# Two attention blocks with pooled keys on one core: parameter vectors loaded as rows, the bias of g carried through W, small PSUM banks for some visits, and the order of the last copies

## The chip, the cores and the metric

One core of one Trainium2 chip runs the whole program. The metric is the device time of one execution in microseconds (us), the median of several runs. The engines named below are PE (TensorE, matrix products; PEld is its weight load), DVE (VectorE), ACT (ScalarE), POOL (GpSimd) and SP (SyncE, which here only issues transfers). PSUM is the memory that PE writes to; the kernel divides its eight banks among three pools.

## The reference

`x` has the shape 4 x 128 x 96 x 96 (batch, channels, height, width), all in fp32. Two layers of the same form follow one another; for each image b with N = 9216 pixels, and with CI = 64:

- g = maxpool2(g_w x + g_b), phi = maxpool2(phi_w x + phi_b), each 64 x 2304 (the pool takes 2 x 2 pixels); theta = theta_w x + theta_b, 64 x 9216
- f = theta^T phi, a 9216 x 2304 matrix of scores; attn = softmax of f over the 2304 keys
- y = attn g^T, back to 64 x 9216
- the output is (W_w y + W_b) * inv + (bn_beta - bn_mean * inv) + x, with inv = bn_gamma / sqrt(bn_var + 1e-5)

The output of layer 0 is the input of layer 1. The parameters of each layer are three matrices 64 x 128 (g_w, phi_w, theta_w), one 128 x 64 (W_w), and vectors: three of 64 elements (g_b, theta_b, phi_b) and five of 128 (W_b, bn_gamma, bn_beta, bn_mean, bn_var). phi_b adds the same to all scores of a pixel and drops out of the softmax. A constant added to g passes the weighted mean of the softmax unchanged.

## The kernel before

`nonlocal_blocks` runs `shifted_blocks`, which takes a fixed shift of 35 from the scores in place of each row's maximum, and then, only if a flag says that the sums of exponentials left the safe range, `general_blocks`. With these inputs the second function isn't run.

**Blocks and pairs.** A block is one image in one layer; `ORDER` (line 41) sets the order of the eight blocks. Each block has nine pairs; a pair is two query tiles of 512 pixels, one on the upper and one on the lower half of the partitions, so there are 72 pairs, numbered through. The 2304 keys make 18 key tiles, two of which are one step; a pair has nine steps. The order of instructions on PE, DVE, ACT and SP is the order of the program (line 77).

**The main loop** (lines 476 to 511). At step t, `scores` (line 276) of the two key tiles of this step: eight products (sixteen instructions, since each fp32 product is two passes) into a large PSUM tile of two banks (pool `ps_sc`, two such tiles), and on ACT the exponential, whose sums DVE adds up (line 292). Then `values` (line 294) of the step before. After the first values of a pair comes the "window": first up to two of the `others`, steps that prepare the next block; then the **visit** (line 429); then the rest of the others; then `normalise`. The visit takes one large tile for two things: the denominators of the pair before (line 313) in its first bank and the theta of the next pair (line 267) in its second; ACT then empties both, the denominators with a running sum (line 323), theta with its bias (line 274). At the fifth step `project` (line 343) multiplies the normalised pair before by W in the two small tiles of one bank each (pool `ps_misc`, used in rotation), and DVE adds the shift and x (line 356).

**The others.** `pooled` (line 200) computes g and phi of 384 pixels, one chunk, in a small tile, and DVE takes their maximum. `spread` (line 242) turns six or three key tiles: on ACT the centred phi, and on PE the transposes of g into a small tile, which DVE adds g's bias to on the way to `gT` (line 235). `key_steps` (line 246) gives the windows of a block their others: with three chunks a window, eight windows have three chunks (two of them a `spread` as well) and the ninth has one `spread` alone. For the second block there are four chunks a window from the third window on, none in the first two, and a `spread` alone in the ninth. In the last block no window has others. The first block's own keys are prepared before the loop and between its first steps.

**The start** (lines 397 to 460). ACT's queue issues g_w, theta_w, theta_b twice as a column, both variances as columns, g_b spread to all partitions, W_w and four rows of vectors. SP's queue issues phi_w and the twelve pieces of the first image, then the parameters of layer 1. PE multiplies the identity eight times as a warm-up (line 445), transposes the weights, and takes chunks 0 to 3, theta of pair 0 (`visit(-1)`), and chunks 4 to 7. ACT takes the square roots of both variances and then loads the table of the exponential. `make_shift` and `make_W` (lines 155 to 169) of layer 0 come at steps 6 and 7, those of layer 1 at steps 18 and 19.

**The end** (`finish`, line 363, for pair 71). `take_denominators` lets DVE take the reciprocals straight out of PSUM and ACT sum the denominators; ACT then copies half of the values (line 368), DVE adds the halves and multiplies, PE projects, and DVE and SP write four pieces. `check` and `result` set the flag in between.

Of the kernel before, what the change touches and what calls it, by code (L numbers as in the profile page):

```python
# [16 lines left out]
P = 128  # L17
# [19 lines left out]
J_WINDOW, J_PROJECT = 0, 4  # L37
CHUNKS = 3
FIRST_CHUNKS, FIRST_GT = 4, 3
WARM = 8  # L40
ORDER = ((0, 0), (1, 0), (0, 1), (2, 0), (1, 1), (3, 0), (2, 1), (3, 1))
SHIFT = 35.0
SUM_MIN, SUM_MAX = 1e-20, 1e30
# [3 lines left out]
def shifted_blocks(ctx: ExitStack, tc: tile.TileContext, x: bass.AP, layers, out: bass.AP, flag):  # L47
# [46 lines left out]
            nc.sync.dma_start(out=xt[:, ts(i, HW // n)], in_=src[:, ts(i, HW // n)])  # L94
        return xt

    def as_column(src):
        return src.rearrange("(c o) -> c o", o=1)

    def as_row(src):  # L100
        return src.rearrange("(o c) -> o c", o=1)

# [9 lines left out]
    class Layer:  # L112


        def __init__(self, l, p):
            self.l, self.p = l, p

        def load_gphi(self, engines):
            self.gphi_nat = prep.tile([2 * CI, C], F32, name=f"gphi_nat_{self.l}")
# [3 lines left out]
        def load_theta(self, engine):  # L123
            self.theta_nat = prep.tile([CI, C], F32, name=f"theta_nat_{self.l}")
            engine.dma_start(out=self.theta_nat, in_=self.p["theta_w"])
            self.theta_b = const.tile([2 * CI, 1], F32, name=f"theta_b_{self.l}")
            for i in range(2):
                engine.dma_start(out=self.theta_b[ts(i, CI), :], in_=as_column(self.p["theta_b"]))

        def load_var(self, engine):  # L130
            self.var = prep.tile([C, 1], F32, name=f"var_{self.l}")
            engine.dma_start(out=self.var, in_=as_column(self.p["bn_var"]))

        def load_g_b(self, engine):
            self.g_b = const.tile([P, CI], F32, name=f"g_b_{self.l}")
            engine.dma_start(out=self.g_b, in_=as_row(self.p["g_b"]).to_broadcast((P, CI)))

        def load_W(self, engine):
            self.W_nat = prep.tile([C, CI], F32, name=f"W_nat_{self.l}")
            engine.dma_start(out=self.W_nat, in_=self.p["W_w"])  # L140
            self.rows = prep.tile([4, C], F32, name=f"rows_{self.l}")
            for i, key in enumerate(("W_b", "bn_gamma", "bn_beta", "bn_mean")):
                engine.dma_start(out=self.rows[i : i + 1, :], in_=as_row(self.p[key]))

        def make_std(self):
            self.std = prep.tile([C, 1], F32, name=f"std_{self.l}")
            nc.scalar.activation(self.std, self.var, AF.Sqrt, bias=eps)

        def make_gphi(self):
            self.gphi = transposed(self.gphi_nat, 2 * CI, C, f"gphiT_{self.l}")  # L150
# [1 line left out]
        def make_theta(self):  # L152
            self.theta = transposed(self.theta_nat, CI, C, f"thetaT_{self.l}")

        def make_shift(self):
            cols = transposed(self.rows, 4, C, f"cols_{self.l}")
            W_b, gamma, beta, mean = (cols[:, i : i + 1] for i in range(4))
            inv = prep.tile([C, 1], F32, name=f"inv_{self.l}")
            nc.vector.reciprocal(inv, self.std)
            nc.vector.tensor_mul(inv, inv, gamma)  # L160
            shift = const.tile([C, 1], F32, name=f"shift_{self.l}")
            nc.vector.tensor_sub(shift, W_b, mean)
            nc.vector.scalar_tensor_tensor(shift, shift, inv, beta, op0=ALU.mult, op1=ALU.add)
            self.shift = shift
            self.W_bn = prep.tile([C, CI], F32, name=f"W_bn_{self.l}")
            nc.vector.tensor_scalar(self.W_bn, self.W_nat, inv, None, ALU.mult)

        def make_W(self):
            self.W = transposed(self.W_bn, C, CI, f"WT_{self.l}", twice=True)

    class Block:

# [54 lines left out]
        def spread_g(self, i):  # L227

            gt = self.gt
            ps = ps_misc.tile([P, QT], F32, tag="misc", name=f"gT_ps_{self.name}_{i}")  # L230
            for j in range(gt):
                nc.tensor.transpose(
                    ps[:, ts(j, CI)], self.gphi[:CI, ts(i * gt + j, KT)], ident[:CI, :CI]
                )
            nc.vector.tensor_tensor(
                self.gT[:, ts(i, gt), :],
                ps[:, : gt * CI].rearrange("p (t c) -> p t c", c=CI),
                self.w.g_b.rearrange("p (o c) -> p o c", o=1).to_broadcast((P, gt, CI)),
                ALU.add,
            )  # L240

        def spread(self, i):
# [13 lines left out]
    class Pair:  # L256
# [14 lines left out]

        def take_theta(self, ps):
            self.th = work.tile([P, QT], F32, tag="theta", name=f"theta_{self.name}")
            nc.scalar.activation(self.th, ps, AF.Identity, bias=self.blk.w.theta_b)  # L274

        def scores(self, k):
            ps = ps_sc.tile([P, PT], F32, tag="sc", name=f"sc_{self.name}_{k}")
# [38 lines left out]
                    )  # L316

        def take_denominators(self, ps):
            self.rc = work.tile([P, QT], F32, tag="rc", name=f"rc_{self.name}", bufs=1)
            if self.last:  # L320
                self.inverses(ps)
            n = self.number
            nc.scalar.activation(  # L323
                self.th if self.last else self.rc, ps, AF.Identity,
                accum_out=dens[:, n : n + 1],
            )

        def inverses(self, src):
            for i in range(QT // P):
# [33 lines left out]
        def finish(self, check, result):  # L363

            n = QT // 2
            halves = work.tile([P, PT], F32, tag="halves", name=f"halves_{self.name}", bufs=1)
            y, half = halves[:, :QT], halves[:, QT:]
            nc.scalar.copy(half, self.av[:, QT:])
            nc.vector.tensor_add(y, self.av[:, :QT], half)
            for i in range(2):  # L370
                nc.vector.tensor_mul(y[:, ts(i, n)], y[:, ts(i, n)], self.rc[:, ts(i, n)])
            self.note()
            pss = [
                ps_sc.tile([P, PT], F32, tag="sc", name=f"W_ps_{self.name}_{i}") for i in range(2)
            ]
            for i in range(2):
                for c in range(2):
                    for h in range(2):
                        nc.tensor.matmul(
                            pss[i][ts(c, CI), h * QT : h * QT + n],  # L380
                            lhsT=self.blk.w.W[ts(h, CI), ts(c, CI)],
                            rhs=y[ts(h, CI), ts(i, n)], start=True, stop=True,
                        )
            check()
            for i in range(2):
                for h in range(2):
                    first = (2 * self.p + h) * QT + i * n
                    dst = self.blk.xt[:, first : first + n]
                    nc.vector.scalar_tensor_tensor(
                        dst, pss[i][:, h * QT : h * QT + n], self.blk.w.shift, dst,  # L390
                        op0=ALU.add, op1=ALU.add,
                    )
                    nc.sync.dma_start(out=self.blk.store[:, first : first + n], in_=dst)
                if i == 0:
                    result()
# [2 lines left out]
    ws[0].load_gphi((nc.scalar, nc.sync))  # L398
    xs = {0: load_x(0, 12)}
    ws[0].load_theta(nc.scalar)  # L400
    for w in ws:
        w.load_var(nc.scalar)
    ws[0].load_g_b(nc.scalar)
    ws[0].load_W(nc.scalar)
    for w in ws:
        w.make_std()
    nc.scalar.preload_act_table(AF.Exp)
    ws[1].load_gphi((nc.sync, nc.sync))
    ws[1].load_theta(nc.sync)
    ws[1].load_g_b(nc.sync)  # L410
    ws[1].load_W(nc.sync)

    blocks = []
# [12 lines left out]
    pairs = [Pair(blk, p, n * NP + p) for n, blk in enumerate(blocks) for p in range(NP)]  # L426
    total = len(pairs) * NB

    def visit(n):

        ps = ps_sc.tile([P, PT], F32, tag="sc", name=f"den_theta_ps_{n}")
        den, th = ps[:, :QT], ps[:, QT:]
        if n > 0:
            pairs[n - 1].denominators(den)
        if n + 1 < len(pairs):
            pairs[n + 1].theta(th)
        if n > 0:
            pairs[n - 1].take_denominators(den)
        if n + 1 < len(pairs):
            pairs[n + 1].take_theta(th)  # L440
# [3 lines left out]
    for i in range(WARM):  # L444
# [7 lines left out]
    b0.pooled(0)  # L452
    b0.pooled(1)
    b0.pooled_2(2)
    b0.spread_phi(0)
    visit(-1)
    b0.pooled(4)
# [8 lines left out]
        2: [lambda: b0.spread_phi(3), lambda: b0.spread_g(3)],  # L466
        4: [lambda: b0.spread_phi(4), lambda: b0.spread_g(4)],
        5: [lambda: b0.spread_phi(5), lambda: b0.spread_g(5)],
        6: [ws[0].make_shift],
        7: [ws[0].make_W],  # L470
        NB: [ws[1].make_gphi, ws[1].make_theta],
        2 * NB: [ws[1].make_shift],
        2 * NB + 1: [ws[1].make_W],
    }
    steps = {}
    for t in range(total + 1):
# [12 lines left out]
        if t:  # L489
            q, j = divmod(t - 1, NB)  # L490
            if j == J_PROJECT and q:
                pairs[q - 1].note()
                pairs[q - 1].project()
            if t <= total:
                for k in range(j * KB, (j + 1) * KB):
                    pairs[q].values(k)
            if t == total - 1:
                visit(len(pairs))
            if t == total:
                break  # L500
            if j == J_WINDOW:
                others = list(steps.pop(q % NP, []))
                for step in others[:2]:
                    step()
                visit(q)
                for step in others[2:]:
                    step()
                if q:
                    pairs[q - 1].normalise()
# [324 lines left out]
```

## Time and profile before

| | us |
|---|---|
| median of 4 runs | 2614.45 (2613.87 to 2615.73) |
| the profiled execution, its own time | 2614.24 |
| its span, first to last instruction | 2612.3 |
| PE busy | 2586.8 |
| DVE busy | 2035.8 |
| ACT busy | 1622.4 |

In a row of the profile, L280 is line 280 of the kernel; then come the engine, the operation, what is written and read by the program's names, the shapes, and the number of instructions. In the view of instructions in order of time, the first number is the start in us after the begin of the span, the second the time from the first start to the last end of the merged instructions. Square brackets show how long the engine stood idle before and what released it. Products overlap in PE's pipeline, so the ends of a group reach into the next one; the distance from one start to the next is the better measure of what a group costs. The granted clock of PE is 0.998 of full speed over the span.

### The profile page before, as it was taken

What the parts mean: (1) busy time and instruction counts of PE and PEld (TensorE: products, weight loads), DVE (VectorE), ACT (ScalarE), POOL (GpSimd) and SP (SyncE); (2) the same over time, 40 slices, a digit from 0 to 9 for tenths busy, and PEclk for the clock granted to TensorE, in tenths of its full rate; (3) what the DMA queues carried; (4) which work ended last, traced back from release to release, by engine and by line L of the source; (5) the groups of instructions that cost most, each with busy time, mean ns of one, the idle gap of its engine ahead of it and who ended that gap; (6) DMA issues with size and microseconds to landing.
All of it is one profiled execution on the core that took longest, in us unless ns stands there. A gap on an engine that the chain in (4) does not pass through costs nothing.

```text
span 2612.3 us, 52223 instructions
## 1 busy us (share of the span) xinstructions
PE 2586.8 (99%) x22838; PEld 908.0 (35%) x22838; DVE 2035.8 (78%) x2067; ACT 1622.4 (62%) x1786; POOL 0.7 (0%) x6
## 2 busy tenths in 40 slices
PE   9999999999999999999999999999999999999998
PEld 3333333333333333333333333333333333333332
DVE  5877778777778777787777887777877778777777
ACT  5666666666666666666666666666666666666664
POOL 0000000000000000000000000000000000000000
PEclk9999999999999999999999999999999999999999
DMA  5000000000000002000000000000000000000000
GB/s 223 1 2 1 1 1 2 1 1 1 1 17 17 9 17 89 2 1 2 1 1 17 17 17 10 17 2 1 1 1 1 17 17 17 17 17 9 17 17 26
DMA packets 11851, 41.50 MB, mean 16 GB/s; under 512 B 2392, under 2 KB 3296, under 8 KB 11616
## 3 DMA queue, kind: packets, MB, share of 16 engines
q1 hardware_dynamic: 10712, 37.95, 3.7%
q8 instruction: 181, 2.97, 0.5%
q14 instruction: 54, 0.44, 0.1%
q10 hardware_dynamic: 904, 0.14, 0.0%
HBM read 19.21 MB, written 18.87 MB: 15 GB/s over the span
## 4 chain that ended last, share of the span: by engine, by line


## 5 line engine op out<-in xcount | busy, mean ns | idle before, releaser
L286 ACT ACTIVATE exp<-sc,nshift 128x1024 f32<-128x1024 f32 x1296 | 1376.3, 1112 | 699.5 <-PE sc L280 699.0
L292 DVE TENSOR_TENSOR sum<-sum,exp 128x1024 f32<-128x1024 f32 x1151 | 1409.3, 1224 | 313.1 <-ACT exp L286 232.0
L280 PE MATMUL sc<-theta,phi 64*64 64x512 f32 x10368 | 1238.4, 591 | 11.4 <-ACT theta L274 6.8
L300 PE MATMUL av<-exp,gT 64*64 64x512 f32 x10368 | 1229.1, 589 | 0.0
L300 PEld LDWEIGHTS av<-exp,gT 64*64 64x64 f32 x10368 | 395.9, 133 | 716.5 <-issue 695.7
L280 PEld LDWEIGHTS sc<-theta,phi 64*64 64x64 f32 x10368 | 384.1, 133 | 732.4 <-issue 646.5
L330 DVE RECIPROCAL rc<-rc 128x128 f32<-128x128 f32 x284 | 240.1, 908 | 13.8 <-ACT rc L323 13.8
L290 DVE TENSOR_TENSOR sum<-exp,exp 128x1024 f32<-128x1024 f32 x72 | 88.2, 1225 | 136.6 <-ACT exp L286 136.6
L323 ACT ACTIVATE rc<-den_theta_ps 128x512 f32<-128x512 f32 x71 | 42.4, 597 | 219.2 <-PE den_theta_ps L267 217.8
L193 DVE TENSOR_REDUCE gphi<-gphi_ps 128x96 f32<-128x384 f32 x192 | 100.2, 552 | 92.9 <-PE gphi_ps L187 92.2
L187 PE MATMUL gphi_ps<-x,gphiT 128*64 128x384 f32 x768 | 146.5, 494 | 0.3 <-DVE gphi L193 0.3
L356 DVE SCALAR_TENSOR_TENSOR x<-W_ps,shift,x 128x512 f32<-128x512 f32 x142 | 99.6, 743 | 0.0
L307 ACT COPY halves<-av 128x1024 f32<-128x1024 f32 x71 | 71.9, 1012 | 32.4 <-PE av L300 32.4
L187 PEld LDWEIGHTS gphi_ps<-x,gphiT 128*64 128x64 f32 x768 | 49.9, 136 | 107.0 <-issue 59.9
L313 PE MATMUL den_theta_ps<-sum,ones 128*64 128x512 f32 x288 | 74.9, 598 | 0.0
L350 PE MATMUL W_ps<-halves,WT 64*64 64x512 f32 x568 | 73.7, 589 | 0.0
L267 PE MATMUL den_theta_ps<-x,thetaT 128*64 128x512 f32 x284 | 73.0, 592 | 0.0
L341 DVE TENSOR_TENSOR halves<-halves,rc 128x512 f32<-128x512 f32 x71 | 49.1, 692 | 2.4
L274 ACT ACTIVATE theta<-den_theta_ps,theta_b 128x512 f32<-128x512 f32 x71 | 48.2, 678 | 4.5 <-PE den_theta_ps L267 4.5
L339 DVE TENSOR_TENSOR halves<-halves 128x512 f32<-128x512 f32 x71 | 48.4, 682 | 0.0
L335 ACT ACTIVATE rc<-rc 128x512 f32<-128x512 f32 x71 | 44.6, 628 | 0.0
L350 PEld LDWEIGHTS W_ps<-halves,WT 64*64 64x64 f32 x568 | 21.7, 133 | 39.2 <-issue 38.9
(67 smaller groups left out, 194.3 us busy)
## 6 DMA issues: line engine op xcount, KB each, us to landing
out_dram<-x SPq DMA_DIRECT2D x35, 512.0 KB, 2.7
x<-in_x_dram SPq DMA_DIRECT2D x18, 768.0 KB, 11.2
x<-in_x_dram SPq DMA_DIRECT2D x12, 384.0 KB, 4.5
out_dram<-x SPq DMA_DIRECT2D x4, 128.0 KB
gphi_nat<-in_L_conv_phi_w_dram SPq DMA_DIRECT2D x2, 32.0 KB
gphi_nat<-in_L_conv_g_w_dram ACTq DMA_DIRECT2D x1, 32.0 KB
theta_nat<-in_L_conv_theta_w_dram ACTq DMA_DIRECT2D x1, 32.0 KB
theta_b<-in_L_conv_theta_b_dram ACTq DMA_DIRECT2D x2, 0.2 KB, 4.7
```

The source lines that it names most:

```text
L187: nc.tensor.matmul(ps[ts(h, CI), :CC], lhsT=self.w.gphi[:, ts(h, CI)], rhs=self.xt[:, ts(r, CC)], start=True, stop=True,)
L193: nc.vector.tensor_reduce(self.gphi[:, ts(r, CC // 4)].rearrange("p (h w) -> p h w", w=W // 2), ps[:, :CC].rearrange("p (h a w b) -> p h w ...
L267: nc.tensor.matmul(ps[ts(h, CI), :], lhsT=self.blk.w.theta, rhs=self.blk.xt[:, ts(2 * self.p + h, QT)], start=True, stop=True,)
L280: nc.tensor.matmul(ps[ts(c, CI), ts(h, QT)], lhsT=self.blk.phi[ts(h, CI), ts(2 * k + c, CI)], rhs=self.th[ts(h, CI), :], start=True, stop= ...
L286: nc.scalar.activation(e, ps, AF.Exp, bias=nshift)
L290: nc.vector.tensor_add(self.sum, self.es[0], e)
L292: nc.vector.tensor_add(self.sum, self.sum, e)
L300: nc.tensor.matmul(self.av[ts(h, CI), ts(r, QT)], lhsT=self.blk.gT[ts(r, CI), k, :], rhs=e[ts(r, CI), ts(h, QT)], start=(k == 0), stop=(k ...
L313: nc.tensor.matmul(ps[ts(h, CI), :], lhsT=ones, rhs=part[:, ts(h, QT)], start=(i == 0), stop=(i == len(parts) - 1),)
L330: nc.vector.reciprocal(self.rc[:, ts(i, P)], src[:, ts(i, P)])
L350: nc.tensor.matmul(pss[h][ts(c, CI), :], lhsT=self.blk.w.W[ts(h, CI), ts(c, CI)], rhs=self.y[ts(h, CI), :], start=True, stop=True,)
L356: nc.vector.scalar_tensor_tensor(dst, pss[h], self.blk.w.shift, dst, op0=ALU.add, op1=ALU.add)
```

## The change

- **Vectors.** `load_var`, `load_g_b`, the columns of theta_b and the rows of `load_W` go. A new function `columns` loads vectors as rows of one tile (a vector of 64 elements twice, side by side) and returns a step that transposes the tile on PE, copies it, and notes each column in the layer's `col`. There are two such tiles: the first with theta_b of layer 0 and both variances (four loads on ACT's queue), the other with the remaining eleven vectors (fourteen loads on SP's queue, after the first image). W_w of layer 0 moves to SP's queue too. A load of ACT's table for the square root stands right after ACT's loads; the square roots and the load of the exponential's table move behind the first chunks.
- **g's bias.** DVE copies g without it; `make_shift` multiplies it by W (scaled) on PE and adds the result to the shift. `make_scale` holds what must come earlier, and is done for both layers at step 6; `make_W` and `make_shift` of layer 0 come at step 7 and those of layer 1 at step 18.
- **Visits.** A visit in a window with fewer than two others takes its denominators and its theta in two small tiles.
- **The end.** ACT's sum of the last denominators moves from `take_denominators` behind the copy of the values.
- The warm-up has five products.

```diff
-WARM = 8
+WARM = 5
...
         def make_std(self):
             self.std = prep.tile([C, 1], F32, name=f"std_{self.l}")
-            nc.scalar.activation(self.std, self.var, AF.Sqrt, bias=eps)
+            nc.scalar.activation(self.std, self.col["bn_var"], AF.Sqrt, bias=eps)
...
+        def make_scale(self):
+            self.inv = prep.tile([C, 1], F32, name=f"inv_{self.l}")
+            nc.vector.reciprocal(self.inv, self.std)
+            nc.vector.tensor_mul(self.inv, self.inv, self.col["bn_gamma"])
             self.W_bn = prep.tile([C, CI], F32, name=f"W_bn_{self.l}")
-            nc.vector.tensor_scalar(self.W_bn, self.W_nat, inv, None, ALU.mult)
+            nc.vector.tensor_scalar(self.W_bn, self.W_nat, self.inv, None, ALU.mult)
 
         def make_W(self):
             self.W = transposed(self.W_bn, C, CI, f"WT_{self.l}", twice=True)
+
+        def make_shift(self):
+            ps = ps_misc.tile([P, QT], F32, tag="misc", name=f"shift_ps_{self.l}")
+            nc.tensor.matmul(
+                ps[:, :1], lhsT=self.W[:CI, :], rhs=self.col["g_b"][:CI, :],
+                start=True, stop=True,
+            )
+            shift = const.tile([C, 1], F32, name=f"shift_{self.l}")
+            nc.vector.tensor_sub(shift, self.col["W_b"], self.col["bn_mean"])
+            nc.vector.scalar_tensor_tensor(
+                shift, shift, self.inv, self.col["bn_beta"], op0=ALU.mult, op1=ALU.add
+            )
+            nc.vector.tensor_add(shift, shift, ps[:, :1])
+            self.shift = shift
+
+    def columns(wanted, name, engine):
+        rows = prep.tile([len(wanted), C], F32, name=f"rows_{name}")
+        for i, (w, key) in enumerate(wanted):
+            n = w.p[key].shape[0]
+            for h in range(C // n):
+                engine.dma_start(out=rows[i : i + 1, ts(h, n)], in_=as_row(w.p[key]))
+
+        def make():
+            cols = transposed(rows, len(wanted), C, f"cols_{name}")
+            for i, (w, key) in enumerate(wanted):
+                w.col[key] = cols[:, i : i + 1]
+
+        return make
...
-            nc.vector.tensor_tensor(
+            nc.vector.tensor_copy(
                 self.gT[:, ts(i, gt), :],
                 ps[:, : gt * CI].rearrange("p (t c) -> p t c", c=CI),
-                self.w.g_b.rearrange("p (o c) -> p o c", o=1).to_broadcast((P, gt, CI)),
-                ALU.add,
             )
...
         def take_denominators(self, ps):
+            self.den, n = ps, self.number
             self.rc = work.tile([P, QT], F32, tag="rc", name=f"rc_{self.name}", bufs=1)
             if self.last:
                 self.inverses(ps)
-            n = self.number
-            nc.scalar.activation(
-                self.th if self.last else self.rc, ps, AF.Identity,
-                accum_out=dens[:, n : n + 1],
-            )
+            else:
+                nc.scalar.activation(self.rc, ps, AF.Identity, accum_out=dens[:, n : n + 1])
...
                 nc.vector.tensor_mul(y[:, ts(i, n)], y[:, ts(i, n)], self.rc[:, ts(i, n)])
+            nc.scalar.activation(
+                self.th, self.den, AF.Identity, accum_out=dens[:, self.number : self.number + 1]
+            )
             self.note()
...
     ws[0].load_theta(nc.scalar)
-    for w in ws:
-        w.load_var(nc.scalar)
-    ws[0].load_g_b(nc.scalar)
-    ws[0].load_W(nc.scalar)
-    for w in ws:
-        w.make_std()
-    nc.scalar.preload_act_table(AF.Exp)
+    first_cols = columns(
+        [(ws[0], "theta_b"), (ws[0], "bn_var"), (ws[1], "bn_var")], "first", nc.scalar
+    )
+    nc.scalar.preload_act_table(AF.Sqrt)
+    rest = ("bn_gamma", "bn_beta", "bn_mean", "W_b", "g_b")
+    other_cols = columns(
+        [(w, key) for w in ws for key in rest] + [(ws[1], "theta_b")], "other", nc.sync
+    )
+    ws[0].load_W(nc.sync)
...
-    def visit(n):
-
-        ps = ps_sc.tile([P, PT], F32, tag="sc", name=f"den_theta_ps_{n}")
-        den, th = ps[:, :QT], ps[:, QT:]
+    def visit(n, shared=True):
+
+        if shared:
+            ps = ps_sc.tile([P, PT], F32, tag="sc", name=f"den_theta_ps_{n}")
+            den, th = ps[:, :QT], ps[:, QT:]
+        else:
+            den = ps_misc.tile([P, QT], F32, tag="misc", name=f"den_ps_{n}")
+            th = ps_misc.tile([P, QT], F32, tag="misc", name=f"theta_ps_{n}")
...
     b0.pooled_2(2)
+    first_cols()
+    for w in ws:
+        w.make_std()
+    nc.scalar.preload_act_table(AF.Exp)
     b0.spread_phi(0)
     visit(-1)
...
-        6: [ws[0].make_shift],
-        7: [ws[0].make_W],
+        6: [other_cols, ws[0].make_scale, ws[1].make_scale],
+        7: [ws[0].make_W, ws[0].make_shift],
         NB: [ws[1].make_gphi, ws[1].make_theta],
-        2 * NB: [ws[1].make_shift],
-        2 * NB + 1: [ws[1].make_W],
+        2 * NB: [ws[1].make_W, ws[1].make_shift],
...
                 others = list(steps.pop(q % NP, []))
                 for step in others[:2]:
                     step()
-                visit(q)
+                visit(q, len(others) > 1)
```

More of the change, by code (lines that the diff above doesn't have):

```diff
@@ L95, in load_x @@
         return xt
-    def as_column(src):
-        return src.rearrange("(c o) -> c o", o=1)
     def as_row(src):
@@ L115, in __init__ @@
         def __init__(self, l, p):
-            self.l, self.p = l, p
+            self.l, self.p, self.col = l, p, {}
         def load_gphi(self, engines):
@@ L125, in load_theta @@
             engine.dma_start(out=self.theta_nat, in_=self.p["theta_w"])
[L126 to L136, printed above, removed]
         def load_W(self, engine):
@@ L140, in load_W @@
             engine.dma_start(out=self.W_nat, in_=self.p["W_w"])
-            self.rows = prep.tile([4, C], F32, name=f"rows_{self.l}")
-            for i, key in enumerate(("W_b", "bn_gamma", "bn_beta", "bn_mean")):
-                engine.dma_start(out=self.rows[i : i + 1, :], in_=as_row(self.p[key]))
         def make_std(self):
             self.std = prep.tile([C, 1], F32, name=f"std_{self.l}")
-            nc.scalar.activation(self.std, self.var, AF.Sqrt, bias=eps)
+            nc.scalar.activation(self.std, self.col["bn_var"], AF.Sqrt, bias=eps)
         def make_gphi(self):
@@ L153, in make_theta @@
             self.theta = transposed(self.theta_nat, CI, C, f"thetaT_{self.l}")
[L155 to L164, printed above, removed]
+        def make_scale(self):
+            self.inv = prep.tile([C, 1], F32, name=f"inv_{self.l}")
+            nc.vector.reciprocal(self.inv, self.std)
+            nc.vector.tensor_mul(self.inv, self.inv, self.col["bn_gamma"])
@@ L273, in take_theta @@
             self.th = work.tile([P, QT], F32, tag="theta", name=f"theta_{self.name}")
-            nc.scalar.activation(self.th, ps, AF.Identity, bias=self.blk.w.theta_b)
+            nc.scalar.activation(self.th, ps, AF.Identity, bias=self.blk.w.col["theta_b"])
         def scores(self, k):
@@ L400, in shifted_blocks @@
     ws[0].load_theta(nc.scalar)
-    for w in ws:
-        w.load_var(nc.scalar)
-    ws[0].load_g_b(nc.scalar)
-    ws[0].load_W(nc.scalar)
-    for w in ws:
-        w.make_std()
-    nc.scalar.preload_act_table(AF.Exp)
+    first_cols = columns(
[7 more added lines that the diff above has]
+    ws[0].load_W(nc.sync)
     ws[1].load_gphi((nc.sync, nc.sync))
     ws[1].load_theta(nc.sync)
-    ws[1].load_g_b(nc.sync)
     ws[1].load_W(nc.sync)
```

## The prediction

> **What bounds the kernel now.** I read the page first: TensorE (PE) is busy 99% of the span, so only PE's gaps can be won, and any wait put in front of PE is paid in full. Then the list of waits, to see who makes PE wait; then PE's rows in order of time around those places; then the first 25 us and the last 20 us on all engines, because there the other engines lead.
>
> ```profile
> span 2612.3 us, 52223 instructions
> PE 2586.8 (99%) x22838; PEld 908.0 (35%) x22838; DVE 2035.8 (78%) x2067; ACT 1622.4 (62%) x1786; POOL 0.7 (0%) x6
> ```
>
> The list of waits has one line on PE that repeats: `PE sc L280 <- ACT theta L274`, 17 times, 6.8 us. One is the start; sixteen are visits. This is such a visit, of the last block (PE's rows; start, length):
>
> ```profile
> 2294.24 1.08 PE L313 MATMUL den_theta_ps<-sum,ones 128*64 128x512 f32 x4
> 2295.15 1.03 PE L267 MATMUL den_theta_ps<-x,thetaT 128*64 128x512 f32 x4
> 2296.11 1.09 PE L280 MATMUL sc<-theta,phi 64*64 64x512 f32 x8
> 2297.54 1.09 PE L280 MATMUL sc<-theta,phi 64*64 64x512 f32 x8 [0.35 <-ACT theta L274]
> 2298.45 1.90 PE L300 MATMUL av<-exp,gT 64*64 64x512 f32 x16
> ```
>
> The second eight score matmuls wait until ACT has emptied the bank that the visit borrowed. Busy ends are modelled, so I count starts: sixteen score matmuls take 2298.45 - 2296.11 = 2.34 us here, and 1.77 after a change of shape with no wait (for instance the group from 55.77 to 57.53). The loss is 0.58 us.
>
> **The change, part by part.** All sums are made against the profiled execution, 2614.24 us for a span of 2612.3 (1.9 lie around it); the median of the runs, 2614.45, is 0.2 above that.
>
> *Visits on the small banks.* Those with fewer than two chunk steps: pairs 0, 1, 8, then 17, 26, 35, 44, 53, 62 (only a gT step), and 63 to 71 (none). Pair 0 has no denominators and shows no wait; 71 has no theta and shows none (its scores take 1.77). So nine visits (1 and 63 to 70) lose 0.58 now. With two small banks of their own, scores alternate over two large banks whose exponentials ended 2 us before; the small banks were last read by the projection, half a pair earlier; ACT can take the denominators about 0.9 us sooner. Nothing is late next: 9 x 0.58 = **-5.2**. Bounds: 0.45 each if the new tile boundary costs a switch, 0.63 if none remains (1.717 per sixteen): -4.0 to -5.6.
>
> The seven visits with a gT step lose more now, but get a new wait: the step's transposes take one small bank, the denominators the other, and theta gets the first one back, which DVE has still to read.
>
> ```profile
> 2259.24 0.58 PE L232 MATMUL gT_ps<-ident,gphi 64*128 64x64 f32 x6
> 2259.75 1.08 PE L313 MATMUL den_theta_ps<-sum,ones 128*64 128x512 f32 x4
> 2260.48 0.55 DVE L235 TENSOR_TENSOR gT<-gT_ps,g_b 128x384 f32<-128x384 f32 x1
> 2260.66 1.03 PE L267 MATMUL den_theta_ps<-x,thetaT 128*64 128x512 f32 x4
> ...
> 2263.18 1.09 PE L280 MATMUL sc<-theta,phi 64*64 64x512 f32 x8 [0.47 <-ACT theta L274]
> ```
>
> DVE's read ends at 2261.03, being queued behind an exp sum of 1.23 us; theta then starts near 2261.10, not 2260.66: +0.44. Behind it on PE stand the scores, for which everyone waits. Removed: sixteen scores of 2.47 (2261.62 to 2264.09) become 1.77: -0.70. Net -0.26 x 7 = **-1.7** (bounds: 0 if the wait is as long as the old one, -4.9 if there is none; I take the DVE row).
>
> *g's bias.* The add becomes a copy: same queue place, and the rows of both kinds (copy of 128 columns 0.29 us, of 64 0.23; the add of 192 0.36, of 384 0.55) lie on one line. 0. But the bias comes back as a matmul whose weights are W transposed, which DVE must first copy out of PSUM, and it follows the transpose at once in PE's order:
>
> ```profile
> 55.54 0.30 PE L105 MATMUL WT_ps<-ident,W_bn 128*64 128x128 f32 x1
> 55.77 0.21 PEld L280 LDWEIGHTS sc<-theta,phi 64*64 64x64 f32 x8
> 56.72 0.28 DVE L107 COPY WT<-WT_ps 64x128 f32<-64x128 f32 x1
> 57.01 0.28 DVE L109 COPY WT<-WT_ps 64x128 f32<-64x128 f32 x1
> ```
>
> Today PE goes on to scores at 55.77; DVE gets to the copy only at 56.72, behind an exp sum. With the change PE waits for the first copy (56.99; it reads the upper half alone), the tiny matmul costs about 0.2 (nearest rows: the cols transpose 0.15 to 0.22, the last test's matmul 0.19), and scores start near 57.28: +1.5. In layer 1 the pair of steps moves to where the cols transpose now stands (97.78): DVE is free of its sum at 98.72, the copy ends at about 98.9, scores start at 99.2 instead of 97.93: +1.25; the WT transpose a step later goes with its change of shape, -0.3. Sum **+2.45**; bounds 2.0 (the matmul free, copies earlier) and 3.1 (both copies waited for, 0.3 more each). W_bn and the scales cost some seven DVE operations of 0.08 to 0.2 us of pitch at t=6, hidden by DVE's wait for exponentials (0.35 there); without that cover 0.2. The sums of the shift end long before the first projection, seven steps later.
>
> *Order of the last copies.*
>
> ```profile
> 2597.19 3.39 DVE L330 RECIPROCAL rc<-den_theta_ps 128x128 f32<-128x128 f32 x4 [2.05 <-PE den_theta_ps L313]
> 2600.68 0.60 ACT L323 ACTIVATE theta<-den_theta_ps 128x512 f32<-128x512 f32 x1 [5.78 <-DVE rc L330]
> 2601.26 0.58 ACT L368 COPY halves<-av 128x512 f32<-128x512 f32 x1
> 2601.87 0.69 DVE L369 TENSOR_TENSOR halves<-av,halves 128x512 f32<-128x512 f32 x1 [1.29 <-ACT halves L368]
> ```
>
> The copy of av stands behind the sum of denominators, which waits for DVE's reciprocals (end 2600.58). Moved ahead, it runs at about 2599.1, when the last value matmuls end, and the add follows the reciprocals at once: 2600.55 instead of 2601.87, **-1.3**. Late next are DVE's reciprocals themselves. The moved sum and the note then end near 2602.35, about when DVE comes to them. Bounds: -0.7 (if the two again meet in one bank) and -1.6.
>
> *The start.* ACT issues six loads instead of twelve, and its first table load (1.28) goes beside the wait. But the square roots now need the transposed rows, whose copy DVE does after the reductions.
>
> ```profile
> 8.31 1.28 ACT L147 ACT_TABLE_LOAD   x1 [8.31 <-DMA g_b<-in_L_conv_g_b_dram]
> 9.61 0.48 ACT L147 ACTIVATE std<-var,eps 128x1 f32<-128x1 f32 x2
> 10.10 1.28 ACT L407 ACT_TABLE_LOAD   x1
> 11.40 0.61 ACT L222 ACTIVATE phi<-gphi,centre 64x384 f32<-64x384 f32 x1
> ```
>
> Reductions end at 9.66; copy of three columns 0.16 (the row of four), square roots at 9.8, table load 10.3 to 11.6, phi at 11.6: 0.2 later than 11.40. Then phi's second part, today bound by DVE's fourth reduction after it (end 13.65), gains: the x load it needs sat on SP for 4.3 us, until 7.58, behind the landing of theta_b's column (SP's own list of waits), and PE stood until 11.05; now PE goes on near 10.8 after a 0.2 us transpose, that reduction ends near 13.3, and the first exponential moves from 14.86 to about 14.7. Everything up to 24 us follows that exponential. I take **-0.1** (-0.5 to +1.3, below). Later parameter loads on SP have until 51 and 62 us, against 21 today: hidden.
>
> Five warm-up products instead of eight end 1.4 us sooner, but PE then waits for theta_w as today (5.61), so nothing is won there. The sixteen warm-up instructions go 0.21 us apart for 128 columns, the first chunks' pairs 0.32 for 384, so the clock doubles between 4.7 and 5.8 us, 3.4 to 4.4 after the first.
>
> [...]
>
> Sum: -5.2 - 1.7 + 2.45 - 1.3 - 0.1 = **-5.85**, so 2608.4 beside the profiled execution, 2608.6 beside the median. I say 2608.5.
>
> **The rivals.**
> 1. *The clock rises late.* If the hole in the warm-up costs another stretch like the first (3.4 us, to about 8.3), chunks 0 to 3, 2.57 us from 5.79, get through half in that time and end 1.25 late, and the whole start with them: 2609.7. For: the hole is real. Against: PE is busy most of the stretch anyway.
> 2. *PE hangs on DVE more than I priced.* Both W copies are waited for (+0.65), and the seven theta waits eat their gain (+1.7): 2610.8. For: DVE is 78% busy, and the order on it is fixed. Against: the rows give both ends.
> 3. *More is won.* The copy is early enough at the seven visits for half of their bound (-1.6) and the last products come before the clock falls (-0.3): 2606.6.
> 4. *Slower.* The transpose of the three rows stands on PE ahead of theta and four chunks. PE gets there at 8.4, and DVE needs it at 9.6; each us of landing after that is paid. Row loads took about 3 us, the columns of theta_b 4.7, the loads of x 11.2 at the median. Issued at 4.2, the last lands at 7 to 9 and costs 0 to 0.4; even 11.2 (15.4) gives 5.8 and brings no change. Only from 20.6 on is it slower by 0.2%: then 2620.
>
> **How the numbers follow.** A measurement of this kernel can tell about 0.2% (5.2 us) from no change; the line is at 2609.2. Forecast 0.58 (0.52 of it below the line, 0.06 above), rival 1 0.16, rival 2 0.12, rival 3 0.10, rival 4 0.03, and 0.01 that the edit does nothing. Faster 0.52 + 0.10 = 0.62; within 0.06 + 0.16 + 0.12 + 0.01 = 0.35; slower 0.03. The range runs from rival 3 to rival 2 with 0.3 of rounding: 2606.3 to 2611.1, leaving out some 0.15.
>
> **What would show it.** In the new profile: `sc <- theta` gone at nine visits (sixteen scores in 1.77), theta 0.4 us late behind the gT copy at seven; PE idle over 1 us before a one-column matmul near 57 and 99 us; the add after the last reciprocals without a wait; the first exponential near 14.7, chunk pairs from 5.79 at 0.32. Wrong if visits still wait on ACT, if those one-column matmuls wait much over 1.5 us, or if the first 24 us change by over 1 us.

## The result and the profile after

| | before | after |
|---|---|---|
| median, us | 2614.13 (53 runs, 2612.71 to 2616.17) | 2609.63 (33 runs, 2608.51 to 2611.45) |
| the profiled execution, its own time | 2614.24 | 2610.71 |
| its span | 2612.3 | 2608.7 |

The ratio is 0.9982, 95% interval 0.9978 to 0.9987: faster by 4.5 us or 0.18%. The forecast was 2608.5, with a line at 2609.2 for "faster by over 0.2%". The time lies within the range, but on the far side of that line, 1.1 us above the forecast and 0.1 from what the first rival gave. In the profiled execution two large misses of opposite sign stand behind that total, so the stages matter more than the sum. PE is as busy as before:

```profile
PE 2586.0 (99%) x22836; PEld 908.7 (35%) x22836; DVE 2036.1 (78%) x2069; ACT 1624.2 (62%) x1786; POOL 0.7 (0%) x6
```

From the starts of PE's groups in the two profiled executions (new lines of the kernel: scores L288, values L308, theta L275, denominators L321, transposes L102, gT L242):

| stage | forecast | measured | how it is read |
|---|---|---|---|
| start | -0.1 | **+3.3** | second group of scores starts at 22.41, not 19.09 |
| shift of layer 0 | +1.5 | +1.6 | from there to pair 1's scores: 41.75, not 40.16 |
| shift of layer 1 | +0.95 | +1.0 | pair 2 takes 38.02, not 36.99 |
| nine visits | -5.2 | -5.2 | pair 1 34.41, not 34.99; pairs 63 to 70 together 270.29, not 274.91 |
| seven visits with a gT step | -1.7 | -1.6 | pairs 8 to 62: 1970.45, not 1972.04 |
| end | -1.3 | **-2.8** | from pair 71's scores to the span's end: 47.3, not 50.1 |
| sum | -5.85 | -3.6 | spans 2608.7 and 2612.3 (the rows above are rounded) |

This profiled execution is one of the longer ones after the change (2610.71 beside a median of 2609.63), so the start's usual loss is smaller: in the two other profiles below with the same start (the shift later; the visit ahead) the second group of scores starts at 20.95 and 20.59, which is 1.9 and 1.5 us later than in the kernel before.

*The visits.* PE's rows of a visit of the last block. The scores that came in two pieces of eight, with a wait for ACT between them, are one group of sixteen, 2301.65 - 2299.88 = 1.77 us:

```profile
2298.93 1.03 PE L275 MATMUL theta_ps<-x,thetaT 128*64 128x512 f32 x4
2299.88 1.95 PE L288 MATMUL sc<-theta,phi 64*64 64x512 f32 x16
2301.65 0.61 PE L308 MATMUL av<-exp,gT 64*64 64x512 f32 x4
```

*A visit behind a gT step* (all engines, in order of time). Theta now waits for DVE's copy out of the bank that it is to get back (end 2265.03); from the start of the denominators to the start of theta it is 1.33 us instead of 0.91, and the scores again take 1.77 instead of 2.47:

```profile
2264.48 0.55 DVE L245 COPY gT<-gT_ps 128x384 f32<-128x384 f32 x1
...
2265.09 1.08 PE L275 MATMUL theta_ps<-x,thetaT 128*64 128x512 f32 x4 [0.25 <-DVE gT L245]
```

*The shift of layer 0.* PE stands behind its own transpose until DVE's first copy ends; the scores, which used to start 0.23 us after the transpose, start 1.82 after it, at 60.67:

```profile
58.85 0.30 PE L102 MATMUL WT_ps<-ident,W_bn 128*64 128x128 f32 x1
60.03 0.28 DVE L104 COPY WT<-WT_ps 64x128 f32<-64x128 f32 x1
...
60.37 0.38 PE L154 MATMUL shift_ps<-cols_other,WT 64*128 64x1 f32 x2 [1.21 <-DVE WT L104]
```

*The start* (PE and ACT). The sixteen instructions of chunks 0 to 3 take 5.3 us (to the next group, 11.98) where they took 2.63, and the transpose of the rows, the square roots (13.22, not the 9.8 forecast) and the first exponential (18.18, not 14.86) all come late with them; theta's weights (transposed at 6.39, after 2.3 us of waiting) came 0.8 late besides. First the chunks in the kernel before, then the changed kernel:

```profile
5.79 2.80 PE L187 MATMUL gphi_ps<-x,gphiT 128*64 128x384 f32 x16
```

```profile
1.36 2.50 PE L459 MATMUL warm_ps<-ident 128*128 128x128 f32 x10 [1.36 <-POOL ident masks.py:199]
...
6.39 0.34 PE L102 MATMUL thetaT_ps<-ident,theta_nat 64*128 64x64 f32 x1 [2.32 <-DMA theta_nat<-in_L_conv_theta_w_dram]
6.66 5.39 PE L197 MATMUL gphi_ps<-x,gphiT 128*64 128x384 f32 x16
11.98 0.26 PE L102 MATMUL cols_first_ps<-ident,rows_first 3*128 3x3 f32 x1
...
18.18 2.12 ACT L294 ACTIVATE exp<-sc,nshift 128x1024 f32<-128x1024 f32 x2
```

*The end.* ACT's copy of the values waits only for PE, DVE's add follows the last reciprocal, and the projection (1.02 us to the next group, 1.91 before) runs at about twice its old pace. First the projection in the kernel before, then the changed kernel:

```profile
2603.17 1.98 PE L379 MATMUL W_ps<-halves,WT 64*64 64x256 f32 x16 [4.15 <-DVE halves L371]
```

```profile
2598.25 0.58 ACT L374 COPY halves<-av 128x512 f32<-128x512 f32 x1 [4.20 <-PE av L308]
2599.66 0.63 DVE L375 TENSOR_TENSOR halves<-av,halves 128x512 f32<-128x512 f32 x1
...
2600.90 1.09 PE L388 MATMUL W_ps<-halves,WT 64*64 64x256 f32 x16 [2.71 <-DVE halves L377]
```

### The profile page after: what moved, and what is told of

The parts are those of the page before. It is cut to its first block, busy times and chain, and to the rows that moved or that the text cites. A ratio compares the mean times of both kernels' runs of the same rounds, so it can differ in the third digit from the quotient of the medians.

```text
span 2608.7 us, 52190 instructions
## 1 busy us (share of the span) xinstructions
PE 2586.0 (99%) x22836; PEld 908.7 (35%) x22836; DVE 2036.1 (78%) x2069; ACT 1624.2 (62%) x1786; POOL 0.7 (0%) x6
## 4 chain that ended last, share of the span: by engine, by line
PE 95%; DVE 2%; ACT 2%; issue 0%; DMA 0%; ACTq 0%; DVEq 0%
PE sc L288 42%; PE av L308 41%; PE gphi_ps L197 5%; PE W_ps L356 2%; PE den_theta_ps L321 2%; PE den_theta_ps L275 2%; ACT exp L294 1%; DVE sum L300 1%; PE theta_ps L275 1%; DVE sum L298 0%; PE den_ps L321 0%; ACT phi L232 0%; DVE centre L230 0%; ACT phi L235 0%; DVE gphi L203 0%
## 5 line engine op out<-in xcount | busy, mean ns | idle before, releaser
L288 PE MATMUL sc<-theta,phi 64*64 64x512 f32 x10368 | 1234.6, 591 | 5.3 <-ACT exp L294 4.6
L308 PE MATMUL av<-exp,gT 64*64 64x512 f32 x10368 | 1229.1, 589 | 0.0
L308 PEld LDWEIGHTS av<-exp,gT 64*64 64x64 f32 x10368 | 395.9, 133 | 716.5 <-issue 696.0
L288 PEld LDWEIGHTS sc<-theta,phi 64*64 64x64 f32 x10368 | 385.8, 133 | 721.3 <-issue 649.2
L332 ACT ACTIVATE rc<-den_theta_ps 128x512 f32<-128x512 f32 x54 | 32.2, 597 | 190.9 <-PE den_theta_ps L275 190.9
L321 PE MATMUL den_theta_ps<-sum,ones 128*64 128x512 f32 x220 | 56.6, 593 | 0.0
L275 PE MATMUL den_theta_ps<-x,thetaT 128*64 128x512 f32 x216 | 55.5, 592 | 0.0
L232 ACT ACTIVATE phi<-gphi,centre 64x768 f32<-64x768 f32 (+1 forms) x27 | 23.2, 859 | 9.1 <-DVE centre L231 8.5
```

The lines of the kernel that those rows point to most:

```text
L275: nc.tensor.matmul(ps[ts(h, CI), :], lhsT=self.blk.w.theta, rhs=self.blk.xt[:, ts(2 * self.p + h, QT)], start=True, stop=True,)
L288: nc.tensor.matmul(ps[ts(c, CI), ts(h, QT)], lhsT=self.blk.phi[ts(h, CI), ts(2 * k + c, CI)], rhs=self.th[ts(h, CI), :], start=True, stop= ...
L308: nc.tensor.matmul(self.av[ts(h, CI), ts(r, QT)], lhsT=self.blk.gT[ts(r, CI), k, :], rhs=e[ts(r, CI), ts(h, QT)], start=(k == 0), stop=(k ...
L321: nc.tensor.matmul(ps[ts(h, CI), :], lhsT=ones, rhs=part[:, ts(h, QT)], start=(i == 0), stop=(i == len(parts) - 1),)
```

## The experiments

Two theories stood for the start. A: the warm-up. Five products end at 3.86, and with the hole until theta's weights come (2.3 us here) PE stays longer at the half pace of its first products. B: the parameter rows and theta's weights land late and the square roots wait for them. For the rest the forecast itself was the theory. The medians are of 5 to 11 runs; each ratio is to runs of the kernel before on the same chip.

### Eight warm-up products in the changed kernel

```diff
-WARM = 5
+WARM = 8
```

> The changed kernel with eight warm-up products again, nothing else. Theory A (the clock): in the changed kernel the first exponential starts at 18.18 us, not 14.86, because the hole after five products keeps PE at half pace until 12 us. Then here chunks 0 to 3 take about 2.6 us again (5.4 with five products), the first exponential starts near 15.0 to 15.6, and the median falls by 2 to 3 us, to about 2607. Rival B (the parameter rows): the start is late because theta_w and the rows land late and the square roots wait for them. Then the first exponential stays at 17 or later and the median near 2609.6.

Measured: 2607.42 (2606.87 to 2609.08), ratio 0.9976 (0.9967 to 0.9985). PE's rows at the start:

```profile
5.74 2.86 PE L197 MATMUL gphi_ps<-x,gphiT 128*64 128x384 f32 x16
8.53 0.22 PE L102 MATMUL cols_first_ps<-ident,rows_first 3*128 3x3 f32 x1
```

The chunks take 2.79 us, the rows are there when PE comes to them (8.53), the square roots run at 9.77 (9.8 forecast), and the first exponential starts at 14.64 (14.7 forecast; 14.86 before). So with the clock in time the loads as rows are no later than the forecast said, and the median is 2.2 us lower (1.9 when each kernel is taken against its own runs of the kernel before). By the trace's semaphore events the last of the four row loads landed at 7.3 in the changed kernel and at 6.3 here, ahead of PE both times. Theory A, not B.

### Five products in the kernel before

```diff
-WARM = 8
+WARM = 5
```

> The kernel before with five warm-up products, nothing else. Theory A: chunks 0 to 3 take about 5 us, the first exponential moves from 14.86 to some 17 us, and the median rises by about 2 us, to 2616. Rival B: nothing moves (14.9, 2614).

Measured: 2615.47, ratio 1.0007 (0.9998 to 1.0016), which alone would decide nothing; medians 1.7 apart. The profile decides: with columns in place of rows, sixteen chunk products take 5.17 us, and the first exponential starts at 17.06. One constant does it (PE's rows; the hole stands in the brackets):

```profile
5.50 0.33 PE L105 MATMUL thetaT_ps<-ident,theta_nat 64*128 64x64 f32 x1 [1.34 <-DMA theta_nat<-in_L_conv_theta_w_dram]
5.76 5.38 PE L187 MATMUL gphi_ps<-x,gphiT 128*64 128x384 f32 x16
```

### Twelve products, none, and five with three more in the hole

```diff
-WARM = 5
+WARM = 12
```

> The changed kernel with twelve warm-up products. [...] If eight are already enough, nothing is gained over eight; if products nine to twelve hold up the weight transposes (they end near 6.4 us), up to 0.5 us is lost.

Measured: 2608.47, ratio 0.9978 (0.9969 to 0.9987). The products hold PE until theta's weights are long there (transposed at 6.99, not 5.3), chunks take 2.73, the first exponential starts at 16.29. More was not better: the products themselves run at half pace (24 instructions from 1.36 to 6.64, 0.22 us each) and hold up what stands behind them. The time is above what either side of the expectation allowed, and the clock rose at 7.07.

```diff
-WARM = 5
+WARM = 0
```

> The changed kernel without any warm-up product. If five products with a hole behind them do nothing for the clock, it rises at 9 to 12.5 us as with five, and the median stays within 0.7 us of 2609.6. [...]

Measured: 2610.12 (2608.69 to 2611.33), ratio 0.9986 (0.9977 to 0.9995). Chunks take 5.18, the first exponential starts at 17.01. The median is 0.5 us above that of five products before a hole, with intervals that overlap, and inside the 0.7 us of the expectation: whether five such products are worth half a us or nothing isn't shown.

```diff
     ws[0].make_gphi()
+    again = ps_sc.tile([P, PT], F32, tag="sc", name="warm_again_ps")
+    for i in range(3):
+        nc.tensor.matmul(again[:, :P], lhsT=ident, rhs=ident, start=True, stop=True)
     ws[0].make_theta()
```

> The changed kernel with its five warm-up products and three more between the transposes of g and phi's weights and of theta's, so that the hole in which PE waits for theta's weights is half filled (three products at half pace take 1.3 us). Eight in all, as in the kernel with eight ahead, where the clock rose at 5.9 and 6.2 us (with five: 9.2 to 12.4 in five profiles). If the hole is what keeps the clock down, it rises by 7 us here, chunks 0 to 3 take under 3.2 us, the first exponential starts at 14.6 to 15.3 and the median is near 2607.4. If only products ahead of the first transpose count, it stays above 9 us and the median near 2609.6.

Measured: 2607.67 (2606.91 to 2608.76), ratio 0.9977 (0.9968 to 0.9986). The hole shrinks to 0.6 us and the chunks run at full pace (5.72 to 8.45; PE's rows). The clock had risen at 4.33, before this rest of the hole began, so the run shows that work in the hole's place is enough, not that a hole of 0.6 us would be harmless:

```profile
3.86 1.06 PE L467 MATMUL warm_again_ps<-ident 128*128 128x128 f32 x6
5.54 0.25 PE L102 MATMUL thetaT_ps<-ident,theta_nat 64*128 64x64 f32 x1 [0.62 <-DMA theta_nat<-in_L_conv_theta_w_dram]
```

### The shift later

```diff
-        7: [ws[0].make_W, ws[0].make_shift],
+        7: [ws[0].make_W],
+        8: [ws[0].make_shift],
...
-        2 * NB: [ws[1].make_W, ws[1].make_shift],
+        2 * NB: [ws[1].make_W],
+        2 * NB + 2: [ws[1].make_shift],
```

> The changed kernel with make_shift one step later in layer 0 and two steps later in layer 1, so that DVE has copied W before PE comes to the one-column product. If the wait for W's copy costs 1.5 and 1.0 us (pair 0 takes 43.1 us against 41.5 before, pair 1 38.0 against 37.0 with its visit's gain taken off), pair 0 takes about 41.7 and pair 1 about 37.2, and the median falls by 2.2 to 2.5 us, to about 2607.3. If the product itself costs most of it, both stay within 0.5 us.

Measured: 2608.53, ratio 0.9979 (0.997 to 0.9988). The stretch from the second group of scores to pair 1 falls from 41.75 to 40.58, pair 2 from 38.02 to 37.23: 2.0 us. The medians lie only 1.1 apart, half of what was expected. In this profile the projection at the end runs at half pace (1.92 us, not 1.02) and pair 44 takes 0.35 longer; whether that explains the median isn't shown. About 0.4 us in layer 0 is left over the kernel before (40.16): 0.31 is the one-column product (from 61.22 to the next group, 61.53), the rest isn't traced. So the wait for W's copy was 1.2 of the 1.6 and 0.8 of the 1.0. DVE copies W while PE is at scores (all engines' rows), and PE comes to the product (61.22) with nothing to wait for:

```profile
58.58 0.28 DVE L104 COPY WT<-WT_ps 64x128 f32<-64x128 f32 x1
...
61.22 0.38 PE L154 MATMUL shift_ps<-cols_other,WT 64*128 64x1 f32 x2
```

### The end alone, in the kernel before

The diff is the two hunks of `take_denominators` and `finish` above.

> The kernel before with only the moved sum of the last denominators. In the changed kernel, the time from the last value products' start to the span's end falls from 15.2 to 12.4 us, 1.4 more than forecast. If the move alone does that, the last W products start 4.7 us after the last value products (6.1 before), run at full pace (sixteen in about 1.0 us, 1.9 before), and the median falls by 2 to 2.7 us. If the pace of the W products and the time of the last landing are chance, the start moves alike, but the W products may take 1.9 and the median falls by about 1.3.

Measured: 2612.12 (2611.47 to 2612.91), ratio 0.9994 (0.9985 to 1.0003); medians 1.7 apart, between the two outcomes expected. The projection starts 4.66 us after the last value products in place of 6.09 (-1.43, forecast -1.3), and takes 1.03 instead of 1.91. That second gain comes and goes: in the profiles with this end, the sixteen instructions of the projection took 1.02 or 1.03 seven times, once 1.27 and once 1.92 (the kernel with the later shift); with the old end they took 1.91, 1.80 and 1.91. So the earlier end mostly, but not always, comes before the clock falls: by the trace's record it fell 0.8 us ahead of the projection in the kernel before, 1.1 after its start here and 2.2 after it in the changed kernel, but 0.3 ahead of it in the kernel with the later shift. From the projection's start to the span's end it took 7.7 to 8.7 in the one, 8.6 to 9.1 in the other.

### The visits alone, in the kernel before

The diff is the hunk of `visit` and its call above.

> The kernel before with only the visits on small banks. Theory: nine visits lose their 0.58 us (sixteen scores after them in 1.77) and seven win 0.23 each, since theta waits for DVE's read of the gT bank: pairs 63 to 69 take 33.8 us instead of 34.36, and the median falls by 6.8 us, to about 2607.3. Rival: ACT takes its work back at the next step, and the median falls by under 4 us.

Measured: 2606.80 (2605.82 to 2608.57), ratio 0.9972 (0.9962 to 0.9983): -7.25. Pair 64 takes 33.78, pairs 63 to 70 270.29, pairs 8 to 62 1970.42, all as in the changed kernel. This one edit is faster than the whole change.

### The visit ahead of the lone gT step

```diff
-                for step in others[:2]:
+                before = 2 if len(others) > 1 else 0
+                for step in others[:before]:
                     step()
                 visit(q, len(others) > 1)
-                for step in others[2:]:
+                for step in others[before:]:
                     step()
```

> The changed kernel with the lone gT step of seven windows behind the visit, not ahead of it. If theta's 0.47 us wait for the gT bank is all that is left there, denominators, theta and scores of these windows lose it and the median falls by 7 x 0.47 = 3.3 us, to about 2606.3. If the transposes then wait for ACT to empty the denominators' bank, or ACT's phi copies delay the exponentials, under 1.5 us is won.

Measured: 2606.22 (2605.11 to 2606.99), ratio 0.9969 (0.9957 to 0.9981): 3.4 below the changed kernel. Pairs 8 to 62 take 1967.18, not 1970.45: 3.3 us, 0.47 a visit. PE runs through: ACT empties the denominators' bank from 2259.74, theta takes PE until 2260.48, and the transposes start without a wait (all engines' rows; PE's has no brackets):

```profile
2259.74 0.60 ACT L332 ACTIVATE rc<-den_ps 128x512 f32<-128x512 f32 x1 [1.39 <-PE den_ps L321]
...
2260.48 0.59 PE L242 MATMUL gT_ps<-ident,gphi 64*128 64x64 f32 x6
```

### The three together

Eight warm-up products, the later shift and the visit ahead, in the changed kernel.

> The changed kernel with eight warm-up products, make_shift later, and the lone gT step behind the visit. If the three terms add up (2.5, 2.3 and 3.3 us), the median is about 2601.5, 0.48% under the kernel before; if they share a wait, 2603 or more.

Measured: 2602.13 (2601.69 to 2603.41, 5 runs), ratio 0.9954 (0.9941 to 0.9968): 7.5 below the changed kernel, against 8.1 for the three terms as expected and 6.7 for the three as their medians came out (2.2, 1.1 and 3.4), and 12 below the kernel before. The stretches are those of the single edits (first exponential 14.81; 40.58; 37.23; 1967.18), so they don't share a wait. It is the fastest kernel of this study.

## Why the prediction was right or wrong

- **PE as the bound, and visits on small banks: right.** Nine times 0.58 and seven times 0.23 (0.26 forecast); shown alone in the kernel before. That theta's wait takes back two thirds of the gain at the seven visits is shown by the kernel that puts the visit first.
- **g's bias: right.** 2.6 for 2.45 forecast; PE waits for the first copy only, as assumed. The run with the later shift shows 2.0 of it to be the wait.
- **Rows for columns: right, once the clock is given.** 14.64 with eight products for the 14.7 forecast (14.56 and 14.81 in two other profiles with the clock in time; 14.83 to 15.18 with columns and eight products). The gain of 0.1 is no larger than this scatter. The late-rows rival didn't come: PE found the rows there at 8.5.
- **The warm-up: wrong. This is the step that failed:** "PE then waits for theta_w as today (5.61), so nothing is won there" priced the edit at 0 in the sum and left +1.25 to a rival at 0.16. In all five profiles with five products and an open hole, or none, the chunks took 4.4 to 5.3 us. The rival was right in its mechanism, and its time, 2609.7, lies 0.1 from the result, but partly by luck: it let half pace end by 8.3, and it lasted to between 9.2 and 12.4; the hole was 1.3 to 2.3 us long. The prediction's own sign of being wrong, the first 24 us changing by over 1 us, came. By medians the edit costs 2.2 (eight against five, changed kernel) and 1.7 (kernel before). The counter-argument, that PE is busy most of the stretch anyway, doesn't hold: PE was busy from about 6 us on, and full pace still came only 3.3 to 5.7 us later. Beside it, theta's weights came 0.8 us late in the one profiled execution (6.39; 5.3 to 5.6 in the ten other profiles in which PE came to them by then). The same loads in the same order stand in six of these, so the new loads don't explain it, and the cause stays open. It makes that profile longer than the median.
- **The end: right in its mechanism, the term too small.** -1.43 for the reorder (-1.3 forecast); the rest is the projection at full pace, which I had put into the rival of more being won, at 0.3, and the last landings. The projection's pace isn't a sure gain: it came in seven of nine profiles.

The sum closes: visits -7.25, end -1.7 and warm-up +1.7 by the medians of the kernel before with one edit, and the shift's +2.6 by its stretches in the profile make -4.6; measured -4.5. The forecast came as near as 1.1 us partly by luck: the visits and the end gave about 0.7 us more than their terms and hid as much of the warm-up's loss.

## What to carry to other kernels

Before shortening a warm-up, look at what PE waits for next: here a hole of 1.3 us or more took nearly all worth from the products ahead of it (without any of them the median was 0.5 us higher, with intervals that overlap), and the first real work then ran at half pace (5.3 us for chunks 0 to 3, not 2.63). A transpose whose result PE itself needs wants other PE work behind it (without it PE waited 1.21 and 0.89 us for the copy here), long enough for the engine that copies it, counted with that engine's queue. And a step that borrows a bank belongs behind the work that others wait for: the same instructions in another order won 3.3 us here.

## What the runs showed of the hardware

In these twelve profiles the moment at which PE's pace doubles (the first entry in the trace's record of the granted clock; in the changed kernel a pair of chunk instructions comes every 0.64 us before it, every 0.32 after) follows the beginning of unbroken PE work. With the warm-up from 1.36 us and PE idle for at most 0.11 us between there and the rise, it came at 4.87, 5.90, 5.33, 5.36 and 6.23 (eight products), 4.33 (five and three) and 7.07 (twelve). With five products and a hole of 1.3 to 2.3 us it came at 12.35, 11.40, 10.21 and 9.22 (four profiles; the expectation above that counts five is wrong), and with none at 10.69, that is 3.3 to 5.7 us after the first chunk product, just as it is 3.0 to 5.7 after the first warm-up product in the other group. The products before the hole count for nothing visible in these times.

What sets the moment within that spread, 3.0 to 5.7 us, isn't shown, nor whether time or the number of products counts: 14 to 26 instructions had started before the rise in the first group, 13 to 20 since the hole in the second. The first rival's +1.25, an estimate from one more stretch of 3.4 us, was too low (1.7 to 2.2 measured).
